# Decoder block on one NeuronCore: four buffers for the down product's integers, convolution sums split between POOL and DVE, the last tile turned on PE, and a new table of wanted times

## The chip, the core and the metric

The kernel runs on one core of a Trainium2 chip. Its engines work side by side, each through its own queue of instructions in a fixed order: PE (matrix products and transposes, results to PSUM), DVE and POOL (elementwise work), ACT (activations, copies, scaling) and SP, which here issues every DMA. POOL works on SBUF alone; DVE and ACT read PSUM too. An instruction starts when it is at the head of its queue and the semaphores it waits for have been raised.

The metric is the device time of one execution in microseconds (us), the median over runs.

## The reference

One decoder block on x of shape (16, 256, 512), in float32. Cut to what matters:

```python
x = x + attn(layernorm(x))            # 16 heads of 32, causal, q/k/v/o projections with bias
x = x + long_conv(ctx, ctx, layernorm(x))   # pairs of ctx rows convolved with a kernel of 512 taps
x = x + ffn(layernorm(x))             # 512 -> 2 x 1408 -> 512, quantized

def quant_dequant(v):                 # per row, for x, h and both weights
    scale = max(max|v| / 127, 1e-8)
    return clip(round(v / scale), -127, 127) * scale
# ffn: gate, up = split(xq @ w1q.T); h = silu(gate) * up; out = quant_dequant(h) @ w2q.T
```

The convolution treats the 16 batches as the long axis and the layer works on 32 groups of 8 channels ("heads" hh, two in each tile). In the quantized part the values that go into the products are small integers, held exactly in bfloat16; "integers" in what follows means these.

## The kernel before

**Order.** Nothing is scheduled by the compiler. Each step of the work (a function with a handful of instructions on one engine) is handed to a planner, class `Plan`, by `pl.add(key, engine, when, took, fn, ...)`: its engine, the time at which it is wanted, a cost, the steps that it comes after (`after`, data; `then`, order only), and the buffers that it takes (`new`) and uses (`use`). `order()` walks through time: whenever an engine is free it starts, of the steps that are ready and whose buffers have room, the one wanted earliest. The list that comes out is the program, and so the order of every engine's queue. The number of buffers of each kind stands in `Plan(...)`; `hq=2` is the ring of the down product's integers. The wanted times are simple formulas, to which the table `shift` adds a correction by kind of step and by stretch of the plan; the stretches are divided at 60, 330, 570, 680 and 1010.

**Attention.** 64 units (16 batches, 4 groups of heads). For each batch the layernorm is split into two half-precision parts, `xh` and `xl` (POOL), which SP turns by DMA transposes (`turn_out`). For each unit PE makes the q and k projections in three products (L617 to L619); ACT and DVE split them again (L725, L730); SP stores them and loads the stacked heads; PE makes the scores (L759), DVE the row extremes (L768), ACT the exponentials (L775), PE transposes (L800) and weighs. Beside this, POOL, ACT and SP prepare the pair products of the convolution (L905, L918, L923) and the integer weights of the quantized part.

**Convolution and quantized part.** 32 tiles of 128 rows, i = 0 to 31 (`NT` is 32). For each half-tile h of a tile, `conv_mm` multiplies on PE (L321 to L323), `conv_mul` multiplies on DVE into one of three buffers `u` (L335, L338, L341), and `conv_sum` adds up in three steps: n = 0, three adds inside `u` (L350, L352, L353); n = 1, three adds into the single buffer `vsum` (L355 to L357); n = 2, one add into `oT` (L361). Steps n = 0 and 1 run on POOL, step 2 on DVE for h = 0 and for the first three tiles, else on POOL. `conv_back` transposes `oT` (PE, L367), `conv_out` adds it to the residual `x2` (DVE, L373). Then comes a norm over ACT, DVE and POOL (L261, L265, L269, L277, L282), the row maximum (DVE, L379 to L381), rounding and casting (ACT, L386, L388) to `xb`, and `ffn_flip`: one DMA transpose from SP to `xq` (L393).

The quantized part of a tile goes through four blocks of columns (384, 384, 384, 256): gate product (PE, L407), scaling (DVE, L414), silu (ACT, L418), times the up scales (L425, on POOL in two halves, for the last two tiles on DVE), up product (PE, L407), times the gate (DVE, L432), row maximum (DVE, L436), its inverse (`up_inv`, four small DVE instructions, L444 to L447), rounding (`up_round`, ACT, L451), casting to `hb` (`up_cast`, ACT, L457), turning by DMA transpose to `hq` (`up_flip`, SP, L463), the down product (PE, L469), its scale and the residual (L478, L487 on DVE; for tiles 28 to 30, `LATE`, L476 on ACT and L483, L484 on POOL), and the store (L491). The last tile (31, `e` in the code) does silu, maximum, rounding, casting and turning block by block, with four DMA transposes; the other tiles do each in one piece.

## Time and profile before

| | us |
|---|---|
| median of three runs | 1176.3 |
| lowest and highest run | 1174.56, 1177.24 |
| the profiled execution, its own time | 1177.95 |
| its span, first to last instruction | 1176.1 |
| POOL add n = 0 (L350, L352, L353), mean of each | 1.278, 0.737, 0.730 |
| POOL add n = 1 (L355, L356, L357), mean of each | 0.937, 0.931, 0.390 |
| the add of n = 2 on POOL (L361), mean | 0.726 |
| the same add on DVE, least, median, most | 0.406, 0.426, 1.477 |
| DMA transpose to landing, xq and hq, median | 2.4, 4.1 |

The profiled execution is a single one, and every duration below is from it; its mean granted TensorE clock is 0.986. Busy shares are averages over stages that differ: attention up to about 631 us (the last transposes at L800 start at 630.9), the convolution and the quantized part after it. A matmul's row carries the length of one instruction; they are pipelined, so 12 gate products of 384 columns take 1.95 us and 11 down products 2.37 us.

### The profile page before, as it was taken

How to read it: one execution, taken by the hardware profiler on the slowest of the kernel's cores; microseconds unless marked ns; L12 is line 12 of the kernel's file. 1: busy time of each engine (PE TensorE's matmuls, PEld its weight loads, DVE VectorE, ACT ScalarE, POOL GpSimd, SP SyncE). 2: the span in 40 equal slices, each digit the busy share in tenths (PEclk: the TensorE clock that was granted, in tenths of full speed). 3: DMA queues.
4: the chain of work that ended last, by engine and by line, in shares of the span. 5: the costliest groups of instructions: out<-in, count | busy, mean ns of one | idle time of the engine just before them, and what ended most of it. 6: DMA issues, size and time to landing. Idle time of an engine off the chain costs nothing.

```text
span 1176.1 us, 25549 instructions
## 1 busy us (share of the span) xinstructions
PE 1083.6 (92%) x8488; PEld 767.0 (65%) x8488; DVE 989.7 (84%) x3165; ACT 839.8 (71%) x2001; POOL 957.2 (81%) x939
## 2 busy tenths in 40 slices
PE   4889989999999999998999999999999999999975
PEld 3666757767667666676666766676776777676632
DVE  5998778888788787886777879999999999999975
ACT  5878878888998888898875455556656665655454
POOL 2585988989899979879513889999999999999971
PEclk9999989999999999999999999999999999999988
DMA  6687787889888779887638855656776667766323
GB/s 223 165 203 230 222 220 231 252 233 242 222 260 230 243 209 260 237 234 213 169 117 291 292 156 156 189 155 186 182 182 165 176 167 171 170 184 177 77 60 69
DMA packets 271106, 229.97 MB, mean 196 GB/s; under 512 B 127257, under 2 KB 225599, under 8 KB 270847
## 3 DMA queue, kind: packets, MB, share of 16 engines
q1 hardware_dynamic: 270975, 228.35, 69.8%
q8 instruction: 67, 1.10, 0.4%
q14 instruction: 64, 0.52, 0.1%
HBM read 124.10 MB, written 75.74 MB: 170 GB/s over the span
## 4 chain that ended last, share of the span: by engine, by line
PE 50%; DVE 20%; ACT 11%; DMA 10%; POOL 4%; issue 3%; SPq 1%; POOLq 0%; ACTq 0%; DVEq 0%
PE g L407 8%; PE c L321 5%; PE c L323 5%; PE c L322 5%; PE d L469 4%; ACT p L775 4%; PE pj_qk L618 3%; PE pj_qk L617 3%; PE pj_qk L619 3%; DMA xlT<-xl 3%; DVE p L768 2%; DVE u L335 2%; DVE s L436 2%; PE pt L800 2%; PE s L759 2%
## 5 line engine op out<-in xcount | busy, mean ns | idle before, releaser
L775 ACT ACTIVATE p<-p,nmax 128x256 f32<-128x256 f32 (+1 forms) x512 | 229.9, 455 | 6.2 <-DVE nmax L768 6.1
L768 DVE CUSTOM_DVE_ANT_0 p<-s,mask,esc 128x128 f32<-128x128 f32 (+1 forms) x512 | 188.1, 410 | 11.8 <-PE s L759 11.4
L321 PE MATMUL c<-bkv,T 128*128 128x288 f16 x640 | 183.9, 287 | 9.4 <-DVE u L341 5.8
L323 PE MATMUL c<-bkv,T 128*128 128x288 f16 x640 | 183.8, 287 | 0.0
L322 PE MATMUL c<-bkv,T 128*128 128x288 f16 x640 | 183.8, 287 | 0.0
L407 PE MATMUL g<-w,xq 128*128 128x384 bf16 (+1 forms) x1024 | 171.5, 313 | 6.4 <-DVE hp L432 3.0
L923 POOL TENSOR_TENSOR kv<-p,kv 128x1152 f16<-128x1152 f32 x64 | 152.0, 2382 | 13.3 <-ACT kv L918 13.1
L905 POOL TENSOR_TENSOR p<-kT 128x1024 f32<-128x1024 f32 x64 | 143.8, 2248 | 2.6
L407 PEld LDWEIGHTS <-xq 128*128 128x128 bf16 x1024 | 99.8, 98 | 58.9 <-issue 7.2
L425 POOL TENSOR_TENSOR g<-g,sw 128x704 f32<-128x704 f32 x60 | 100.6, 1698 | 8.2 <-ACT g L418 8.2
L775 ACT ACTIVATION_READ_ACCUMULATOR p<-p,nmax 128x1 f32 x512 | 101.0, 197 | 0.0
L759 PE MATMUL s<-st 96*128 96x128 f16 (+1 forms) x512 | 85.1, 247 | 13.9 <-DVE nmax L768 10.1
L335 DVE TENSOR_TENSOR u<-c,qT 128x512 f32<-128x512 f32 x128 | 87.4, 682 | 11.3 <-PE c L323 9.0
L730 DVE SCALAR_TENSOR_TENSOR qkhl<-pj_qk,bias,qkhl 128x256 f16<-128x256 f32 x128 | 59.7, 478 | 40.2 <-ACT qkhl L725 30.8
L725 ACT ACTIVATE qkhl<-pj_qk,bias 128x256 f16<-128x256 f32 x128 | 60.1, 470 | 45.9 <-PE pj_qk L619 38.0
L469 PE MATMUL d<-w,hq 128*128 128x512 bf16 x352 | 85.8, 393 | 7.7 <-DVE s L445 4.3
L451 ACT ACTIVATE hp<-hp,s 128x1408 f32<-128x1408 f32 (+2 forms) x35 | 47.7, 1369 | 54.2 <-DVE s L447 54.1
L350 POOL TENSOR_TENSOR u<-u 128x512 f32<-128x512 f32 x64 | 81.8, 1278 | 5.4 <-DVE u L335 5.4
L321 PEld LDWEIGHTS <-T 128*128 128x128 f16 x640 | 62.8, 98 | 29.1 <-DVE u L341 7.7
L800 PE MATMUL pt<-idf,p 128*128 128x128 f32 x520 | 79.7, 277 | 2.3 <-ACT t L808 1.3
L918 ACT CAST kv<-p 128x1152 f16<-128x1152 f32 x64 | 73.5, 1149 | 11.0 <-POOL p L909 5.9
L786 POOL TENSOR_SCALAR lb<-lsum 128x256 f32<-128x256 f32 x64 | 26.0, 406 | 64.1 <-DVE lsum L782 40.0
(220 smaller groups left out, 3323.9 us busy)
## 6 DMA issues: line engine op xcount, KB each, us to landing
kv_d<-kv SPq DMA_DIRECT2D x64, 576.0 KB, 4.1
bkv<-kv_d SPq DMA_DIRECT2D x64, 576.0 KB, 4.1
qk_d<-qkhl SPq DMA_DIRECT2D x64, 256.0 KB, 3.3
st<-qk_d SPq DMA_DIRECT2D x256, 64.0 KB, 2.5
T<-pad_d SPq DMA_DIRECT2D x64, 256.0 KB, 5.0
x_d<-xt SPq DMA_DIRECT2D x32, 256.5 KB, 3.6
bx<-x_d SPq DMA_DIRECT2D x32, 256.5 KB, 3.9
xt<-in_x_dram SPq DMA_DIRECT2D x16, 512.0 KB, 4.0
```

The lines of the kernel that those rows point to most:

```text
L321: nc.tensor.matmul(reg, T[:, 0, d:d + P], kv[:, mi, 0, :], start=mi == 0, stop=False)
L322: nc.tensor.matmul(reg, T[:, 0, d:d + P], kv[:, mi, 1, :], start=False, stop=False)
L323: nc.tensor.matmul(reg, T[:, 1, d:d + P], kv[:, mi, 0, :], start=False, stop=mi == li)
L335: nc.vector.tensor_tensor(ap(u, uo, [[UW, 2], [64, 4], [1, 64]]), ap(pc, 0, [[512, 2], [64, 4], [1, 64]]), ap(qT, qo, [[96, 2], [8, 4], [1 ...
L407: nc.tensor.matmul(pg[:, :c.stop - c.start].rearrange("p (r o) -> p r o", o=P), t["xq"][:, kc, :], w1[:, (o + c.start) // P:(o + c.stop) / ...
L469: nc.tensor.matmul(pd.rearrange("p (r o) -> p r o", o=P), t["hq"][:, ic, :], w2[:, :, ic, :], start=ic == 0, stop=ic == IC - 1)
L759: nc.tensor.matmul(ps[:, hh, :nk], stk[:, 0, 2 * h2 + hh, qc * P:(qc + 1) * P], stk[:, 1, 2 * h2 + hh, :nk], start=True, stop=True)
L768: nc.vector.tensor_tensor_reduce(out=prs[b, g][qc][:, h, :], in0=ps[:, hh, :nk], in1=mask2[:, P - qc * P:2 * P], op0=ALU.add, op1=ALU.min, ...
L775: nc.scalar.activation(pr[:, h, :], pr[:, h, :], AF.Exp, scale=-1.0, bias=nmax[:, qc, h:h + 1], accum_out=lsum[:, qc, h:h + 1])
L800: nc.tensor.transpose(pt[:, j, :], src, idf)
L905: nc.gpsimd.tensor_tensor(ap(p, 0, [[NKV, 4], [64, 4], [1, 64]]), ap(kT, o, [[96, 4], [0, 4], [1, 64]]), ap(kT, o, [[96, 4], [8, 4], [1, 6 ...
L923: nc.gpsimd.tensor_tensor(kv[:, :, 1, :], p, kv[:, :, 0, :], ALU.subtract)
```

## The change

Four things. The ring of `hq` has four buffers instead of two. `conv_sum` asks a function `sum_on` for its engine: step n = 0 of the second half-tile of tiles 0 to 3 goes from POOL to DVE, and step n = 1 of the last half-tile too; when n = 0 and n = 1 are on different engines, n = 1 no longer waits for n = 0. In the last tile, the input's integers and the down product's are turned by transposes on PE into PSUM and copied to SBUF, instead of by DMA; of the four column blocks the odd ones are rounded, cast and copied on DVE, the even ones on ACT. The table of wanted times is replaced as a whole (the boundaries stay), and the bias maximum at the start is wanted later. A bfloat16 identity is made at the start.

```diff
@@ -147,6 +147,8 @@
 
     idf = cst.tile([P, P], F32, name="idf")
     make_identity(nc, idf)
+    idb = cst.tile([P, P], BF16, name="idb")
+    nc.vector.tensor_copy(idb, idf)
 
     mask2 = cst.tile([P, 2 * P], F32, name="mask2")
     nc.gpsimd.memset(mask2, 0.0)
@@ -195,6 +197,7 @@
     NT = len(tiles)
     UB = 3
     LATE = range(NT - 4, NT - 1)
+    EARLY = 4
 
     ts = [dict() for _ in tiles]
 
@@ -342,9 +345,13 @@
             ap(u, uo + 256, [[UW, 2], [32, 2], [1, 32]]), ap(pc, 256, [[512, 2], [0, 2], [1, 32]]),
             ap(qT, qo + 32, [[96, 2], [32, 2], [1, 32]]), ALU.mult)
 
+    def sum_on(i, h, n):
+        dve = (n == 2 and (h == 0 or i < 3)) or (n == 0 and h and i < EARLY) or (n == 1 and h and i == NT - 1)
+        return "DVE" if dve else "POOL"
+
     def conv_sum(i, h, n):
         u = ts[i]["u", h]
-        g = nc.gpsimd
+        g = nc.gpsimd if sum_on(i, h, n) == "POOL" else nc.vector
         if n == 0:
             a = ap(u, 0, [[UW, 4], [1, 128]])
             g.tensor_tensor(a, a, ap(u, 128, [[UW, 4], [1, 128]]), ALU.add)
@@ -358,7 +365,7 @@
         else:
             if h == 0:
                 ts[i]["oT"] = cv.tile([P, 4, P], F32, tag="oT", bufs=3, name=f"oT{i}")
-            (g if h and i > 2 else nc.vector).tensor_tensor(ts[i]["oT"][:, :, 64 * h:64 * h + 64], ap(u, 0, [[UW, 4], [1, 64]]), vs[:, :, 0:64], ALU.add)
+            g.tensor_tensor(ts[i]["oT"][:, :, 64 * h:64 * h + 64], ap(u, 0, [[UW, 4], [1, 64]]), vs[:, :, 0:64], ALU.add)
 
     def conv_back(i):
         t = ts[i]
@@ -386,6 +393,17 @@
         nc.scalar.activation(xn, xn, AF.Copy, bias=RND, scale=t["s"][:, 1:2])
         t["xb"] = ff.tile([P, D], BF16, tag="xb", bufs=2, name=f"xb{i}")
         nc.scalar.activation(t["xb"], xn, AF.Copy, bias=-RND)
+
+    def ffn_turn(i):
+        t = ts[i]
+        t["pt"] = ps_sd.tile([P, 512], BF16, tag="sd", name=f"sd_x{i}")
+        for kc in range(KC):
+            nc.tensor.transpose(t["pt"][:, kc * P:(kc + 1) * P], t["xb"][:, kc * P:(kc + 1) * P], idb)
+
+    def ffn_keep(i):
+        t = ts[i]
+        t["xq"] = ff.tile([P, KC, P], BF16, tag="xq", bufs=5, name=f"xq{i}")
+        nc.vector.tensor_copy(t["xq"].rearrange("p k s -> p (k s)"), t["pt"])
 
     def ffn_flip(i):
         t = ts[i]
@@ -448,18 +466,41 @@
 
     def up_round(i, n):
         t, c = ts[i], parts(i)[n]
-        nc.scalar.activation(t["hp"][:, c], t["hp"][:, c], AF.Copy, bias=RND, scale=t["s"][:, 3:4])
+        if n % 2:
+            nc.vector.tensor_scalar(t["hp"][:, c], t["hp"][:, c], t["s"][:, 3:4], RND, ALU.mult, ALU.add)
+        else:
+            nc.scalar.activation(t["hp"][:, c], t["hp"][:, c], AF.Copy, bias=RND, scale=t["s"][:, 3:4])
 
     def up_cast(i, n):
         t, c = ts[i], parts(i)[n]
         if n == 0:
             t["hb"] = ff.tile([P, I], BF16, tag="hb", bufs=2, name=f"hb{i}")
-        nc.scalar.activation(t["hb"][:, c], t["hp"][:, c], AF.Copy, bias=-RND)
+        if n % 2:
+            nc.vector.tensor_scalar(t["hb"][:, c], t["hp"][:, c], -RND, None, ALU.add)
+        else:
+            nc.scalar.activation(t["hb"][:, c], t["hp"][:, c], AF.Copy, bias=-RND)
+
+    def up_turn(i, n):
+        t, c = ts[i], parts(i)[n]
+        if n == 0:
+            t["pt"] = ps_c.tile([P, 2048], BF16, tag="c", name=f"c_h{i}")
+        for j in range(c.start, c.stop, P):
+            nc.tensor.transpose(t["pt"][:, j:j + P], t["hb"][:, j:j + P], idb)
+
+    def up_keep(i, n):
+        t, c = ts[i], parts(i)[n]
+        if n == 0:
+            t["hq"] = ff.tile([P, IC, P], BF16, tag="hq", bufs=4, name=f"hq{i}")
+        dst = t["hq"].rearrange("p r s -> p (r s)")[:, c]
+        if n % 2:
+            nc.vector.tensor_copy(dst, t["pt"][:, c])
+        else:
+            nc.scalar.copy(dst, t["pt"][:, c])
 
     def up_flip(i, n):
         t, c = ts[i], parts(i)[n]
         if n == 0:
-            t["hq"] = ff.tile([P, IC, P], BF16, tag="hq", bufs=2, name=f"hq{i}")
+            t["hq"] = ff.tile([P, IC, P], BF16, tag="hq", bufs=4, name=f"hq{i}")
         nc.sync.dma_start_transpose(t["hq"][:, c.start // P:c.stop // P, :], t["hb"][:, c])
 
     def down_mm(i):
@@ -1032,11 +1073,11 @@
         T = 8.8
         pl = Plan(xt=XB, xn=1, xh=2, xl=2, xhT=2, xlT=2, v=2, pj=2, qk=3, st=STB, s=2, pr=2, lb=2, pt=3, tt=2, av=1,
                   lt=2, ah=2, ct=1, cr=2, kT=2, p=2, kv=2, qw=3, qb=2, qt=2, x1=5, q=2, qT=4, sd=1, kv2=3, c=2, u=UB, oT=3, x2=8, xn2=2, xb=2, xq=5, ac=3,
-                  g1=3, hp=2, hb=2, hq=2, o1=2)
+                  g1=3, hp=2, hb=2, hq=4, o1=2)
 
         pl.add("bi", "SP", -100, 1.1, bias_in, late=2.0, dma=0.3)
         pl.add("bm", "PE", -99, 0.1, bias_turn, late=0.2, after=["bi"], new=[("pt", "b")])
-        pl.add("bx", "DVE", -98, 0.7, bias_max, late=0.1, after=["bm"], use=[("pt", "b")])
+        pl.add("bx", "DVE", -66, 0.75, bias_max, late=0.1, after=["bm"], use=[("pt", "b")])
         for n, nm in enumerate(names):
             j = n // 2
             pl.add(("pi", nm), "SP", -80 + 10 * n, 0.55, proj_in, nm, late=1.5, dma=3.3)
@@ -1260,8 +1301,9 @@
                            after=[("cm", hh, l2), ("bk", i, 1), ("cz", hh % UB)], then=[("cu", hh, 0) if l2 else ("cu", hh - 1, 1)],
                            new=[u] * (1 - l2), use=[c, u, qT])
                 for n in range(3):
-                    pl.add(("cs", hh, n), "DVE" if n == 2 and (h == 0 or i < 3) else "POOL", w + 6 + 2.5 * n, (2.85, 2.37, 0.69 if h else 0.45)[n], conv_sum, i, h, n, late=0.08,
-                           after=[("cu", hh, 1)] if n == 0 else [("cs", hh, n - 1)], then=[("cs", hh - 1, 2)],
+                    on = sum_on(i, h, n)
+                    pl.add(("cs", hh, n), on, w + 6 + 2.5 * n, ((2.85, 2.37, 0.69) if on == "POOL" else (2.3, 2.0, 0.45))[n], conv_sum, i, h, n, late=0.08,
+                           after=[("cu", hh, 1)] + [("cs", hh, m) for m in range(n) if n == 2 or sum_on(i, h, m) == on], then=[("cs", hh - 1, 2)],
                            new=[oT] * (n == 2 and h == 0), use=[u] + [oT] * (n == 2))
             pl.add(("co", i), "PE", t + 22, 0.44, conv_back, i, late=0.2, after=[("cs", 2 * i + 1, 2)], new=[("sd", ("o", i))], use=[oT])
             pl.add(("cx", i), "DVE", t + 23, 0.67, conv_out, i, late=0.1, after=[("co", i), "ff"], new=[x2], use=[("sd", ("o", i)), x1])
@@ -1269,7 +1311,11 @@
             root(i, "f", t + 24, [("cx", i)], xn, 0.1)
             pl.add(("fm", i), "DVE", t + 27, 0.98, ffn_top, i, late=0.1, after=[("fq", i)], use=[xn, x2])
             pl.add(("fo", i), "ACT", t + 28, 1.29, ffn_round, i, late=0.1, after=[("fm", i)], new=[("xb", i)], use=[xn])
-            pl.add(("ft", i), "SP", t + 30, 1.23, ffn_flip, i, late=1.2, dma=0.8, after=[("fo", i)], new=[("xq", i)], use=[("xb", i)])
+            if e:
+                pl.add(("fd", i), "PE", t + 30, 0.35, ffn_turn, i, late=0.2, after=[("fo", i)], new=[("sd", ("x", i))], use=[("xb", i)])
+                pl.add(("ft", i), "DVE", t + 30.5, 0.45, ffn_keep, i, late=0.1, after=[("fd", i)], new=[("xq", i)], use=[("sd", ("x", i))])
+            else:
+                pl.add(("ft", i), "SP", t + 30, 1.23, ffn_flip, i, late=1.2, dma=0.8, after=[("fo", i)], new=[("xq", i)], use=[("xb", i)])
             xq, g1, hp, hb, hq, o1 = ("xq", i), ("g1", i), ("hp", i), ("hb", i), ("hq", i), ("o1", i)
             g = t + (34 if e else 38)
             np = NC if e else 1
@@ -1286,12 +1332,18 @@
                        after=[("gm", i, 1, n), ("gu", i, n if e else 0)], then=[("um", i, 0)] * (n > 0), new=[hp] * (n == 0), use=[("ac", (i, 1, n)), g1, hp])
             for n in range(np):
                 pl.add(("gl", i, n), "ACT", g + 7 + n, 1.37 * k + 0.16 * e, gate_silu, i, n, late=0.1, after=[("gs", i, n if e else NC - 1)], use=[g1])
-                pl.add(("gu", i, n), "POOL" if i < NT - 2 else "DVE", g + 8 + n, (3.4 if i < NT - 2 else 1.5 + 0.3 * e) * k, gate_ups, i, n, late=0.05,
+                pl.add(("gu", i, n), "POOL" if i < NT - 2 else "DVE", g + 8 + n, (3.3 if i < NT - 2 else 1.5 + 0.3 * e) * k, gate_ups, i, n, late=0.05,
                        after=[("gl", i, n), ("fv", 1)], use=[g1])
                 pl.add(("ut", i, n), "DVE", g + 15 + n, 1.54 * k + 0.08 * e, up_top, i, n, late=0.1, after=[("um", i, n if e else NC - 1)], use=[hp])
-                pl.add(("uq", i, n), "ACT", g + 18 + n, 1.37 * k + 0.15 * e, up_round, i, n, late=0.1, after=[("ui", i)], use=[hp])
-                pl.add(("ub", i, n), "ACT", g + 19 + n, 1.28 * k + 0.1 * e, up_cast, i, n, late=0.1, after=[("uq", i, n)], new=[hb] * (n == 0), use=[hp, hb])
-                pl.add(("uf", i, n), "SP", g + 20 + n, 1.2 if e else 1.45, up_flip, i, n, late=1.2, dma=2.1 * k, after=[("ub", i, n)], new=[hq] * (n == 0), use=[hb, hq])
+                q = "DVE" if n % 2 else "ACT"
+                pl.add(("uq", i, n), q, g + 18 + n, 0.35 if n % 2 else 1.37 * k + 0.15 * e, up_round, i, n, late=0.1, after=[("ui", i)], use=[hp])
+                pl.add(("ub", i, n), q, g + 19 + n, 0.35 if n % 2 else 1.28 * k + 0.1 * e, up_cast, i, n, late=0.1, after=[("uq", i, n)], then=[("ub", i, 0)] * (n > 0), new=[hb] * (n == 0), use=[hp, hb])
+                if e:
+                    c = ("c", ("h", i))
+                    pl.add(("ud", i, n), "PE", g + 20 + n, 0.28, up_turn, i, n, late=0.2, after=[("ub", i, n)], then=[("ud", i, n - 1)], new=[c] * (n == 0), use=[hb, c])
+                    pl.add(("uf", i, n), q, g + 20.5 + n, 0.4, up_keep, i, n, late=0.1, after=[("ud", i, n)], then=[("uf", i, 0)] * (n > 0), new=[hq] * (n == 0), use=[c, hq])
+                else:
+                    pl.add(("uf", i, n), "SP", g + 20 + n, 1.45, up_flip, i, n, late=1.2, dma=2.1, after=[("ub", i, n)], new=[hq] * (n == 0), use=[hb, hq])
             pl.add(("ui", i), "DVE", g + 17, 0.76 + 0.2 * e, up_inv, i, late=0.1, after=[("ut", i, n) for n in range(np)], use=[x2])
             pl.add(("dm", i), "PE", g + 25, 2.38, down_mm, i, late=0.2, after=[("uf", i, n) for n in range(np)] + [("fw", 4)],
                    new=[("ac", (i, 2))], use=[hq])
@@ -1305,102 +1357,104 @@
 
         bounds = (60,330,570,680,1010)
         shift = {-            ("bi", 2): (-7.9, -13.9, -6, -15.4, -13.3, -3.2),
-            ("bk", 3): (4.3, -0.6, -0.5, -0.8, -0.8, 0.9),
...
+            ("bi", 2): (0.8, 5.7, 3, 5.9, 1.9, 8.6),
+            ("bk", 3): (14.4, 12.2, -4.6, 11.1, 15.6, 13.5),
...
```

## The prediction

> **What bounds the kernel now.** I read the busy shares first, then the busy time by stage, then the tail engine by engine in order of time, then the waits of PE. Busy shares over the whole span:
>
> ```profile
> PE 1083.6 (92%) x8488; PEld 767.0 (65%) x8488; DVE 989.7 (84%) x3165; ACT 839.8 (71%) x2001; POOL 957.2 (81%) x939
> ```
>
> PE is idle for 1176.1 - 1083.6 = 92.5 us. The stages (columns: stretch, length, then busy time and instructions of PE, PEld, DVE, ACT, POOL, granted clock, DMA share, GB/s) say where:
>
> ```profile
> 0.00:60.00 60.00, 39.22 (x294) 31.27 (x295) 43.30 (x148) 42.32 (x85) 24.53 (x29) 1.00 0.67 194
> 60.00:200.00 140.00, 127.67 (x1103) 91.43 (x1102) 117.11 (x446) 116.72 (x354) 114.51 (x93) 0.98 0.77 221
> 200.00:330.00 130.00, 124.23 (x1084) 89.86 (x1083) 108.14 (x424) 117.67 (x359) 119.30 (x95) 1.00 0.86 239
> 330.00:450.00 120.00, 111.26 (x964) 80.55 (x963) 97.34 (x381) 106.23 (x312) 108.96 (x89) 1.00 0.83 235
> 450.00:570.00 120.00, 110.76 (x960) 79.00 (x959) 92.09 (x352) 101.03 (x294) 101.38 (x79) 0.99 0.78 224
> 840.00:920.00 80.00, 79.65 (x573) 56.47 (x572) 75.13 (x195) 48.81 (x68) 76.47 (x88) 1.00 0.67 172
> 1100.00:1140.00 40.00, 33.34 (x199) 19.89 (x198) 32.69 (x80) 22.09 (x26) 33.46 (x38) 0.91 0.26 51
> 1140.00:1176.00 36.00, 21.86 (x108) 10.08 (x106) 21.28 (x49) 15.26 (x22) 9.81 (x8) 0.89 0.29 64
> ```
>
> Between 840 and 920 PE is busy 99.6%: there nothing that leaves PE's work as it is can help. The idle time sits in the start (20.8 us), in attention (60 to 570: 510 - 473.9 = 36.1 us), in 620 to 760 (10.5 us: 140 less 129.5), and in the tail, 1100 to 1176 (20.8 us). The tail in order of time (start, length, what; in brackets the idle time before and its cause):
>
> ```profile
> 1135.79 0.74 DVE L373 SCALAR_TENSOR_TENSOR x<-sd_o,rsall,bx 128x512 f32<-128x512 f32 x1
> ...
> 1160.36 0.21 DVE L447 TENSOR_SCALAR s<-s 128x1 f32<-128x1 f32 x1
> 1170.33 0.76 DVE L478 SCALAR_TENSOR_TENSOR d<-d,s,sw 128x512 f32<-128x512 f32 x1 [9.76 <-PE d L469]
> 1171.60 0.69 DVE L487 TENSOR_TENSOR o<-d,x 128x512 f32<-128x512 f32 x1 [0.51 <-DMA out_dram<-o]
> ```
>
> From the last tile's residual (1136.45) to its inverse maximum (1160.57) DVE idles 2 us of 24.1: DVE bounds this piece. From 1160.57 to 1170.33 everything waits on one chain. ACT and PE show it:
>
> ```profile
> 1161.89 1.11 ACT L451 ACTIVATE hp<-hp,s 128x384 f32<-128x384 f32 x2
> 1162.90 0.93 ACT L457 ACTIVATE hb<-hp 128x384 bf16<-128x384 f32 x2
> 1163.72 1.01 ACT L451 ACTIVATE hp<-hp,s 128x384 f32<-128x384 f32 x2
> 1164.63 0.82 ACT L457 ACTIVATE hb<-hp 128x384 bf16<-128x384 f32 x2
> ```
> ```profile
> 1169.69 0.60 PE L469 MATMUL d<-w,hq 128*128 128x512 bf16 x2 [0.51 <-DMA hq<-hb]
> ```
>
> ACT ends casting at 1165.45, but PE ends at 1170.29: 4.8 us are DMA transposes landing one behind the other.
>
> **Part 1, the last turn (tail after 1160.57).** Before: 1176.1 - 1160.57 = 15.5 us. Now, from the inverse on: two roundings and two casts on ACT, 1.11 + 0.93 = 2.0, while DVE does the other four (its nearest row is L414, 128x384 in 0.55, so at most 2.2). Then ACT has tile 30's o1 scale (0.67) in front of its copies; the 11 transposes (four of L367 take 0.60 to 0.66, so about 1.7) run meanwhile, behind the down products of tiles 29 and 30. Two copies on ACT: between 0.37 (128x256, L841) and 0.57 (128x512, L808), say 0.47 each, 0.95. Hops between engines, four at about 0.1: 0.4. Last three down products 0.82. Sum 4.9, then the same end as before: 0.76 + 0.69, and 3.8 from 1172.29 to the end of the span. That gives 10.2; I take 11.0, since tile 29's scale stood before the roundings for 1.3 us and may again. Gain 4.5; bounds: 2.0 (that wait stays, and all 11 products wait for the last copy, 1.6 more) and 5.3. The stores of tiles 29 and 30 leave SP earlier than before, as six DMA transposes are gone from its queue; the ring of two o1 buffers held the last add 0.5 us before and can again. The input's turn (one DMA transpose, median 2.4 to landing, against 0.66 + 0.69 for transposes and copy, L810) I cost at nothing: DVE has over 10 us of queue before that copy. Without this cover it gains 1.0.
>
> **Part 2, the tail before 1160.57.** The new order of the queues puts more of tiles 28 to 30 ahead of the last tile. Counting DVE's queue between x2 of tile 31 and its inverse, at this trace's durations (four scalings 1.8, four products with the gate 1.75, the up scales 1.65 or 1.75, a row maximum 1.53, an inverse 0.76, norm maximum 1.0): before 22.1 us, after 19.4 with the new copy of 0.6, since tile 29's and 30's scalings and a quarter of tile 29's products have moved ahead of x2. Idle was 2.0; I allow 2.5, as the last tile now runs more alone. That is 24.1 to 21.9, a gain of 2.2. Ahead of it POOL, from the last add of n = 2 on DVE (1109.77 before) to the end of oT31 (1134.53), has 24.8 us before and, counted from its new queue, 22.3 (one step n = 1 less; 11 us of up scales stay). DVE has about 24 in the same stretch, so only 0.8 of it counts. Gain 3.0; bounds -1 (DVE's two extra SBUF adds each held, below) and 6 (POOL's and DVE's savings in full, no new idle time).
>
> **Part 3, tiles 0 to 3.** Four steps n = 0 leave POOL: 4 x (1.28 + 0.74 + 0.73) = 11.0 us. On DVE the three adds take at least 0.68 + 0.41 + 0.41 = 1.5 (L335 for 512 elements, L361 for 256), so 6 us. But the same add on DVE takes two lengths:
>
> ```profile
> 652.23 1.39 DVE L361 TENSOR_TENSOR oT<-u,vsum 128x256 f32<-128x256 f32 x1
> 664.26 0.43 DVE L361 TENSOR_TENSOR oT<-u,vsum 128x256 f32<-128x256 f32 x1
> ```
> ```profile
> 652.08 1.26 POOL L350 TENSOR_TENSOR u<-u 128x512 f32<-128x512 f32 x1
> 663.13 1.27 POOL L350 TENSOR_TENSOR u<-u 128x512 f32<-128x512 f32 x1
> ```
>
> The long one started just behind a POOL add and ended with it; the short one started as another POOL add was ending (664.40). So each of the 12 moved adds can be held by up to 1.0 us: DVE pays 6 to 18 us, and between 640 and 720, where these tiles run, it has 14.9 us idle (POOL 10, PE 6.6). PE's own waits for `u` are 4.3 us here. I take a gain of 1.0; bounds -4 (18 less 14.9, and conv_mul, which PE waits for, queued behind the held adds) and 4 (those 4.3 us).
>
> The Trainium skill's page "SBUF — State Buffer", section "Who interferes with whom", says more than these rows: a DVE instruction with two SBUF inputs and a POOL instruction that reads SBUF exclude each other for a whole instruction. Then POOL too stands still during the moved adds and wins only half of what it hands over; by that rule this part would be worth nothing, and the total one microsecond less.
>
> **Part 4, four hq buffers.** Nothing. No row of SP's waits names the down product as what held a transpose; PE's 3.4 us of waiting for hq are all in the last tile. Bounds 0 and 1.
>
> **Part 5, the new order elsewhere.** Attention has the same instructions. On PE's queue I counted, at the trace's pitches, the work between a unit's last projection and its first score: median 17.6 us before, 17.0 after, least 9.7 and 8.9; between last score and first transpose 6.0 and 6.6. Nothing separates the two orders. At the start the second batch's input is loaded and split earlier, but k's norm comes behind one more cast (1.0): I allow a gain of 1. For the rest the four stretches between 60 and 570 show how far one order varies: PE idles 8.8, 4.4, 7.3 and 7.7%, a scatter of 1.9%, which is 2.4 us in a stretch and 4.8 over four independent ones. Value 1.0, bounds -9 and 11 (two scatters each way).
>
> **Sum.** 4.5 + 3.0 + 1.0 + 0 + 1.0 = 9.5. The profiled execution took 1177.95 (span 1176.1, 1.85 around it), so 1168.5 for it; it stands 1.65 above the median, so 1167 for a median.
>
> **The rivals.**
> - *Slower: the new order starves the projections.* In attention the longest kind of DMA wait is this:
>
> ```profile
> PE pj_qk L618 <- DMA xlT<-xl: 6.4, 7, 2.3
> ```
>
> 6.4 us in 7 waits, the longest 2.3. If the 15 batches after the first all wait the longest, that is 34.5, 28 more. It decides from (9.5 + 2.4 + 6.4) / 15 = 1.2 us in each batch; half way between that point and the worst the time would be 1167 + 20 = 1187. For it: SP's queue is one, and every store moved ahead of the xl transpose delays PE. Against it: the number of units still to be stored behind that transpose averages 0.7 before and 1.0 after, no worse. Chance 0.20.
> - *No change: the tail keeps its length.* DVE stays the bound, its held adds and the longer idle time of a lone last tile eat part 2, part 1 gives its 2.0 and the rest cancels: 1176.3 - 2.0 = 1174 to 1176. For it: DVE is already at 88% from 1135 to 1161. Against it: the DMA landings do go. Chance 0.10, half of it within 0.2%.
> - *Faster still: the order also fills attention.* If all of 60 to 570 idled as the best stretch does (4.4%), 36.1 would become 22.7, and 1167 - 13.4 = 1153. For it: one stretch does it with POOL and ACT over 90% busy. Against it: the counts above. Chance 0.20.
>
> **How the numbers follow.** Forecast 1167 with 0.50. Its own range: half bounds of 1.7, 3.5, 4 and 7 (0.8 of part 5's) add in squares to 9, so 1158 to 1176. The full range takes in the faster rival and about a third of the slower: 1153 to 1182. A measurement here can tell about 0.2%, 2.4 us. Faster: 0.50 less 0.02, 0.20, and 0.05 of the middle rival, 0.73; within 0.2%: 0.02 and 0.05, 0.07; slower 0.20.
>
> **What would show it.** From the last tile's inverse to the end of the span 10 to 12 us instead of 15.5 (part 1; wrong if over 13.5), from its x2 to the inverse 20 to 23 instead of 24.1 (part 2), the moved adds on DVE with lengths spread from 0.4 to 1.5 (part 3), no wait gone at SP (part 4), PE's busy time between 60 and 570 within 5 us of 473.9 (part 5). The prediction is wrong if PE's idle time in attention moves by more than 12 us, or if DVE from 640 to 720 has no idle time left and PE's waits for `u` grow.

## The result and the profile after

The changed kernel takes 1159.65 us (median of four runs, 1158.62 to 1164.23), the kernel before 1176.49 in the same session: a ratio of 0.9867 with a 95% interval of [0.9837, 0.9896], some 16 us. The profiled execution of after took 1164.23, the longest of its four; its span is 1162.4 us against 1176.1, and the mean granted clock 0.993 against 0.986. The busy shares over the span, then the same stages as before (columns as in the prediction):

```profile
PE 1076.4 (93%) x8503; PEld 766.8 (66%) x8503; DVE 1015.8 (87%) x3188; ACT 838.0 (72%) x1999; POOL 947.5 (82%) x924
```
```profile
0.00:60.00 60.00, 42.30 (x316) 33.97 (x317) 43.92 (x160) 45.33 (x92) 27.03 (x30) 1.00 0.69 203
60.00:200.00 140.00, 128.36 (x1106) 91.72 (x1104) 118.31 (x446) 119.55 (x362) 117.83 (x95) 0.99 0.83 225
200.00:330.00 130.00, 125.35 (x1104) 91.86 (x1102) 109.30 (x426) 117.38 (x355) 118.87 (x96) 1.00 0.82 236
330.00:450.00 120.00, 109.99 (x959) 79.32 (x958) 98.25 (x388) 102.49 (x305) 101.30 (x83) 0.99 0.85 237
450.00:570.00 120.00, 114.84 (x997) 82.38 (x995) 95.23 (x365) 107.92 (x320) 108.79 (x85) 1.00 0.82 234
840.00:920.00 80.00, 79.30 (x565) 55.54 (x563) 75.93 (x193) 46.34 (x63) 75.25 (x87) 1.00 0.64 173
1100.00:1140.00 40.00, 27.49 (x159) 15.80 (x156) 37.43 (x81) 20.32 (x23) 22.75 (x24) 0.91 0.20 41
1140.00:1162.00 22.00, 13.57 (x76) 6.72 (x76) 14.83 (x31) 9.16 (x15) 7.69 (x6) 0.94 0.36 80
```

PE does 3.1 us more in the first 60 us and 4.6 more between 60 and 570 (478.5 against 473.9). From 840 to 920 it stays busy 99.1%, against 99.6. In the tail DVE is now the full engine: 37.4 of 40 us, where it had 32.7. PE's 27.5 against 33.3 is no loss of work: the span is 13.7 us shorter, so this window lies nearer to its end; in the 40 us that end 36 us before the end of each span PE is busy 32.3 and was 33.3, and DVE 37.8 and was 32.7.

Landmarks tell better than shares where the 13.7 us between the spans come from. Each is the start of a named instruction, in us:

| | before | after | gain |
|---|---|---|---|
| first unit weighed (first DVE write of `al`; L853, now L894) | 63.5 | 60.4 | 3.1 |
| last unit weighed | 636.3 | 624.2 | 12.1 |
| first conv matmul (L321, now L324) | 633.7 | 621.6 | 12.1 |
| last conv matmul, counted from the first | 482.2 | 481.5 | 0.7 |
| last inverse (first instruction), counted from the last conv matmul | 43.6 | 45.9 | -2.3 |
| end, counted from that inverse | 16.6 | 13.4 | 3.2 |

So nearly all of it is won before the convolution starts, the long middle is as it was, and the tail gives back in front of the inverse most of what it wins behind it. The tail on DVE, in order of time (start, length, what): the last residual, the end of the last inverse, the last down product's scale and residual.

```profile
1128.81 0.74 DVE L380 SCALAR_TENSOR_TENSOR x<-sd_o,rsall,bx 128x512 f32<-128x512 f32 x1
...
1149.85 0.21 DVE L465 TENSOR_SCALAR s<-s 128x1 f32<-128x1 f32 x1
...
1156.99 0.76 DVE L519 SCALAR_TENSOR_TENSOR d<-d,s,sw 128x512 f32<-128x512 f32 x1 [1.16 <-PE d L510]
1157.84 0.69 DVE L528 TENSOR_TENSOR o<-d,x 128x512 f32<-128x512 f32 x1
```

From the inverse's end (1150.06) to the span's end are 12.3 us, where there were 15.5. From the residual (ends 1129.48) to the inverse's end are 20.6, where there were 24.1. The residual itself, however, ends 26.4 us after the start of the last conv matmul, where it ended after 20.5.

PE's waits between 60 and 560 us (us in total, times, longest) do not get shorter everywhere:

```profile
PE pj_qk L659 <- DMA xlT<-xl: 10.7, 6, 3.7
PE pj_qk L658 <- ACT qkhl L766: 6.9, 9, 1.1
PE s L800 <- DVE nmax L809: 6.6, 14, 1.7
```

The wait for the transposed `xl` rose from 6.4 to 10.7 us, the one for ACT's `qkhl` from 4.8 to 6.9, and the one for `nmax` fell from 8.4 to 6.6; the rows that went are many small ones (the wait for the stacked heads `st` was 2.0, for DVE's `t` 2.0 and 1.1, for `qkhl` on DVE 2.3, now 1.0).

### The profile page after: what moved, and what is told of

It is laid out like the page before. It is cut to its first block, busy times and chain, and to the rows that moved or that the text cites. A ratio compares the mean times of both kernels' runs of the same rounds, so it can differ in the third digit from the quotient of the medians.

```text
span 1162.4 us, 25593 instructions
## 1 busy us (share of the span) xinstructions
PE 1076.4 (93%) x8503; PEld 766.8 (66%) x8503; DVE 1015.8 (87%) x3188; ACT 838.0 (72%) x1999; POOL 947.5 (82%) x924
## 4 chain that ended last, share of the span: by engine, by line
DVE 32%; PE 31%; POOL 13%; ACT 9%; DMA 8%; issue 5%; SPq 2%; DVEq 0%; POOLq 0%; ACTq 0%
DVE hp L450 4%; PE g L425 4%; ACT p L816 3%; DVE s L454 3%; DVE u L338 3%; DVE p L809 3%; PE pj_qk L659 3%; PE pj_qk L658 3%; PE pj_qk L660 3%; DMA xlT<-xl 2%; DVE u L341 2%; PE c L324 2%; PE c L326 2%; PE c L325 2%; POOL g L443 2%
## 5 line engine op out<-in xcount | busy, mean ns | idle before, releaser
L816 ACT ACTIVATE p<-p,nmax 128x256 f32<-128x256 f32 (+1 forms) x512 | 230.0, 454 | 11.3 <-DVE nmax L809 10.7
L324 PE MATMUL c<-bkv,T 128*128 128x288 f16 x640 | 183.2, 286 | 9.4 <-issue 3.2
L425 PE MATMUL g<-w,xq 128*128 128x384 bf16 (+1 forms) x1024 | 169.1, 315 | 13.1 <-DVE o L528 6.3
L771 DVE SCALAR_TENSOR_TENSOR qkhl<-pj_qk,bias,qkhl 128x256 f16<-128x256 f32 x128 | 59.9, 478 | 33.5 <-ACT qkhl L766 21.0
L357 POOL TENSOR_TENSOR u<-u 128x512 f32<-128x512 f32 x60 | 76.9, 1282 | 9.6 <-DVE u L338 9.6
L510 PE MATMUL d<-w,hq 128*128 128x512 bf16 x352 | 80.9, 379 | 3.8 <-DVE hp L450 3.0
L324 PEld LDWEIGHTS <-T 128*128 128x128 f16 x640 | 62.6, 98 | 29.1 <-DVE u L344 5.9
L659 PE MATMUL pj_qk<-xlT,wq_hi 128*128 128x256 f16 x256 | 70.5, 275 | 10.7 <-DMA xlT<-xl 10.7
L658 PE MATMUL pj_qk<-xhT,wk_hi 128*128 128x256 f16 x256 | 70.0, 273 | 7.3 <-ACT qkhl L766 6.9
```

The source lines that it names most:

```text
L324: nc.tensor.matmul(reg, T[:, 0, d:d + P], kv[:, mi, 0, :], start=mi == 0, stop=False)
L425: nc.tensor.matmul(pg[:, :c.stop - c.start].rearrange("p (r o) -> p r o", o=P), t["xq"][:, kc, :], w1[:, (o + c.start) // P:(o + c.stop) / ...
L658: nc.tensor.matmul(ps, lh, rh, start=first, stop=False)
L659: nc.tensor.matmul(ps, lh, rl, start=False, stop=False)
L816: nc.scalar.activation(pr[:, h, :], pr[:, h, :], AF.Exp, scale=-1.0, bias=nmax[:, qc, h:h + 1], accum_out=lsum[:, qc, h:h + 1])
```

## The experiments

Each run stands beside runs of the kernel before on the same chip. The table has the ratio to that kernel, and from the profiled execution the start of the first conv matmul, the length of the conv stretch (first to last conv matmul), the way from the last conv matmul to the first instruction of the last inverse, and from there to the end.

| run | ratio and 95% interval | first conv | conv stretch | to inverse | to end |
|---|---|---|---|---|---|
| before | 1 | 633.7 | 482.2 | 43.6 | 16.6 |
| after | 0.9867 [0.9837, 0.9896] | 621.6 | 481.5 | 45.9 | 13.4 |
| e1_old_table | 1.0204 [1.0175, 1.0233] | 631.5 | 499.0 | 52.3 | 14.7 |
| e2_table_only | 1.0056 [1.0034, 1.0079] | 614.5 | 504.9 | 45.0 | 15.9 |
| e3_sum_pool | 0.9871 [0.9849, 0.9894] | 619.0 | 481.4 | 46.0 | 13.4 |
| e4_dma_last | 0.9892 [0.9873, 0.9911] | 614.2 | 481.9 | 45.9 | 16.6 |
| e5_attn_table | 1.0072 [1.0049, 1.0096] | 615.2 | 500.9 | 48.3 | 15.9 |
| e6_new_conv | 1.0166 [1.0149, 1.0183] | 633.5 | 497.7 | 49.2 | 14.4 |
| e7_early_on_pool | 0.9860 [0.9838, 0.9882] | 615.2 | 481.7 | 46.7 | 13.3 |
| e8_ring_two | 0.9876 [0.9827, 0.9926] | 619.9 | 479.8 | 46.7 | 13.3 |
| e9_order_only | 0.9901 [0.9869, 0.9934] | 616.1 | 481.6 | 46.3 | 16.6 |
| e10_tail_new | 0.9849 [0.9825, 0.9873] | 617.7 | 479.6 | 42.8 | 14.2 |
| e11_tail_two | 0.9800 [0.9777, 0.9822] | 615.2 | 479.4 | 40.8 | 12.4 |
| e12_start_only | 0.9962 [0.9939, 0.9985] | 627.6 | 482.0 | 43.3 | 16.6 |

### The table of wanted times, whole and in parts

e1 gives the changed kernel the old table:

```diff
-            ("bi", 2): (0.8, 5.7, 3, 5.9, 1.9, 8.6),
+            ("bi", 2): (-7.9, -13.9, -6, -15.4, -13.3, -3.2),
...
```

> The changed kernel with the wanted times of the kernel before (its shift table; steps new in the change get no shift); all else as changed. Theory (the new order of start and attention brings some 12 us of the 13.7 between the profiled spans): 1170 to 1177 us, and the first conv matmul starts within 4 us of the 633.7 of before, against 621.6 after. Rival (the early sums on DVE, the ring of four or the turn on PE bring the gain): 1158 to 1163, with the first conv matmul near 622. The old table was made for other steps, so a time above 1180 speaks against neither.

Measured: 1198.6 us. The first conv matmul is at 631.5, as the theory said; but the conv stretch grew by 17 us, which neither theory had (a time above 1180 had been allowed for, as speaking against neither). e2 is the other half, the kernel before with the new table (the same lines the other way round):

> The kernel before with the new wanted times alone: no sum moved, two buffers for the down product's integers, the last tile turned by DMA. Theory (the table's first stretches bring some 12 us): 1162 to 1167 us, first conv matmul between 619 and 625. Rival (the table needs the other parts with it): 1172 to 1180, first conv matmul above 629.

Measured: 1181.15 us. Attention gains even more than in the changed kernel, 614.5 against 633.7 before, and the conv stretch loses 22.7 us. So in both, attention's length follows the table, and the total does not: the theory's total was wrong by 14 us or more. e5 and e6 divide the table by its columns, that is by stretches of the plan.

```diff
# e5, in the kernel before: three new columns, three old ones
-            ("bi", 2): (-7.9, -13.9, -6, -15.4, -13.3, -3.2),
+            ("bi", 2): (0.8, 5.7, 3, -15.4, -13.3, -3.2),
...
# e6, in the changed kernel: three old columns, three new ones
-            ("bi", 2): (0.8, 5.7, 3, 5.9, 1.9, 8.6),
+            ("bi", 2): (-7.9, -13.9, -6, 5.9, 1.9, 8.6),
...
```

> The kernel before with the new wanted times in the table's first three columns alone (planned times below 570); the three later columns, the sums, the ring and the last tile's transfers as before. Theory (the new order of start and attention is worth 12 to 19 us by itself, and the later columns fit only the code that they were made for): first conv matmul between 613 and 622 against 633.7, conv stretch 480 to 484 us as before, so 1156 to 1165 us. Rival (attention's gain needs the later columns too, or is given back in the conv stretch as in the run with the whole table): first conv matmul above 628, or a conv stretch above 490, and 1172 to 1185 us.

> The changed kernel with the first three columns of the old table and the last three of the new one. Theory (the early columns are the gain, the later ones fit the moved sums): first conv matmul 629 to 634, conv stretch 480 to 485 us, end 58 to 60 us after the last conv matmul, so 1168 to 1176 us. Rival (the conv stretch's order was fitted to the new order of attention, too): a conv stretch above 488 us, and 1177 to 1195.

Measured: 1186.41 and 1196.95 us. Attention is at 615.2 with the new early columns and at 633.5 with the old ones, in whichever code. The conv stretch is long again in both, 500.9 and 497.7: here the rivals were right, though both times came out just above their ranges. Where the conv stretch loses, PE waits longer for DVE's products into `u`, which read the conv product's PSUM buffer and so free it. Two views: the conv matmuls of e5 with their first and last start, and PE's waits over e5's conv stretch.

```profile
L321 PE MATMUL c<-bkv,T x640: 282/286/448, 615.2 to 1116.1; 128*128 128x288 f16 x160
```
```profile
PE c L321 <- DVE u L341: 10.9, 8, 3.8
PE c L321 <- DVE rn_f L265: 5.0, 3, 2.5
```

The same wait in the kernel before, on which e5 is built, and in the changed kernel, each over its own conv stretch:

```profile
PE c L321 <- DVE u L341: 5.8, 8, 1.4
```
```profile
PE c L324 <- DVE u L344: 3.2, 4, 1.8
```

10.9 us against 5.8 and 3.2, and 5.0 more that the profile puts down to an instruction of DVE's norm. In e1, e2 and e6 this wait is 9.8, 10.7 and 11.6 us. In e5 the two rows make up 10 of the 19 us; the rest is spread over smaller ones.

e12 changes the first column alone in the kernel before:

> The kernel before with the new wanted times in the table's first column alone (planned times below 60): the start's order, with the old columns behind it. Read by the first conv matmul, since a mixed table costs the conv stretch 15 to 23 us in every run so far. Theory (the start brings the 3 us by which the first unit is earlier, the columns of attention the rest): first conv matmul at 629 to 632 us against 633.7 before and 615 with three new columns. Rival (the start's order sets the rhythm of the units, and all of the gain comes from it): 613 to 622. The time: 1175 to 1200 either way.

Measured: 1170.68 us, first conv matmul at 627.6, 6.1 us earlier, between the two cases and nearer the theory; the first unit is weighed at 59.9 against 63.5, so 3.6 of the 6.1 are there by 60 us. The times agree: 0.9962 [0.9939, 0.9985] is 2 to 7 us, and not all of the gain. (e12 keeps the bias maximum where it was and has no second identity, so the start's gain is not theirs.) The assumption in the expectation, that a mixed table always costs the conv stretch, is wrong: 482.0. Counting in the programs fits this. Of DVE's 741 steps of the convolution and the quantized part, e12 has none in another order than the kernel before; e5 has 333 out of their old order, e2 420, and the changed kernel itself 380. All kernels in which this part has the complete order of before, or of after, have a conv stretch of 479 to 482 us; the four new mixtures have 498 to 505. Why these two orders are good and four others bad was not tried.

e9 keeps the changed kernel's order and undoes its other parts in their places:

```diff
# e9
-        g = nc.gpsimd if sum_on(i, h, n) == "POOL" else nc.vector
+        g = nc.gpsimd if sum_on(i, h, n) == "POOL" or n < 2 else nc.vector
...
-        if n % 2:
+        if False:
...
-            if e:
+            if False:
                 pl.add(("fd", i), "PE", ...)
...
-tag="hq", bufs=4
+tag="hq", bufs=2
```

> The changed kernel with all of its other parts undone in their places: the early sums and the last middle sum on POOL, two buffers for the integers, the last tile rounded on ACT and turned by DMA; the order of the work is the changed kernel's wherever the steps are the same. Theory (the whole gain is the order's, 12 us of it ahead of the first conv matmul, and the three other parts together bring at most 4 us): 1160 to 1166 us, first conv matmul 613 to 622, conv stretch 480 to 484 us. Rival (the parts each bring something that the others cover when one is undone alone): above 1168 us.

Measured: 1162.31 us, ratio 0.9901 [0.9869, 0.9934], first conv matmul 616.1, conv stretch 481.6, each as the theory said. 1.0% of the 1.33% (11.6 of some 16 us; by the interval 8 to 15) is the order's. This is the run that settles where the gain comes from; that it comes before the conv stretch is e1, e2, e5 and e6 together.

### The last tile's turn

e4 undoes the turn on PE, as in e9, and with it the split of the last tile's rounding and casting (all four blocks on ACT again); the sums and the ring stay as changed.

> The changed kernel with the last tile's integers of both products turned by DMA as before, all blocks rounded and cast on ACT, ring of four and all else kept. Theory (the turn on PE saves 3 us after the inverse and 3.5 before it): 5 to 7 us slower than the changed kernel, 1165 to 1167, with 15 to 16 us from the start of the last inverse to the end, against 12.3, and 23.5 to 24.5 from x2 to the inverse, against 20.6. Rival (the tail's order, not the transfer, sets these lengths): 0 to 2 us slower, the two lengths within 1 us of the changed kernel's.

Measured: 1161.49 us, 0.25% above the changed kernel, about 2.9 us, with intervals that overlap. The lengths show it clearly. (The expectation's 15 to 16 and 12.3 are counted from the inverse's end, not from its start.) From the inverse's end to the end of the span 15.5 us against 12.3; from the residual to the inverse's end 20.6 in both. The split brings none of it: the last cast ends 4.2 us behind the inverse in e4, with all blocks on ACT, and 4.1 in the changed kernel. So the turn of the down product's integers is worth 3.2 us, and the turn of the input nothing. PE at the end of e4, and at the end of after:

```profile
1146.99 0.82 PE L510 MATMUL d<-w,hq 128*128 128x512 bf16 x3 [2.54 <-DMA hq<-hb]
1149.31 2.74 PE L510 MATMUL d<-w,hq 128*128 128x512 bf16 x6 [1.49 <-DMA hq<-hb]
1152.53 0.60 PE L510 MATMUL d<-w,hq 128*128 128x512 bf16 x2 [0.49 <-DMA hq<-hb]
```
```profile
1151.69 0.34 PE L488 MATMUL c_h<-idb,hb 128*128 128x128 bf16 x3 [0.24 <-ACT hb L481]
1152.97 0.51 PE L488 MATMUL c_h<-idb,hb 128*128 128x128 bf16 x6 [0.94 <-DVE hb L479]
1154.24 0.29 PE L488 MATMUL c_h<-idb,hb 128*128 128x128 bf16 x2 [0.76 <-DVE hb L479]
1154.37 2.58 PE L510 MATMUL d<-w,hq 128*128 128x512 bf16 x11
```

In e4 the down products wait three times for a transfer (2.54, 1.49, 0.49). In after the turns wait for the casts on DVE (0.94, 0.76), which end late for a reason of their own: the rows of DVE and of POOL there.

```profile
1150.10 2.54 DVE L470 TENSOR_SCALAR hp<-hp,s 128x384 f32<-128x384 f32 x2
1152.57 1.62 DVE L479 TENSOR_SCALAR hb<-hp 128x384 bf16<-128x384 f32 x2
```
```profile
1149.88 1.27 POOL L524 TENSOR_TENSOR o<-o,sw 128x512 f32<-128x512 f32 x1 [6.83 <-ACT o L517]
1151.23 1.27 POOL L525 TENSOR_TENSOR o<-o,x 128x512 f32<-128x512 f32 x1
1152.70 1.34 POOL L524 TENSOR_TENSOR o<-o,sw 128x512 f32<-128x512 f32 x1 [0.20 <-ACT o L517]
```

Two roundings take 2.54 us and two casts 1.62; the first pair ends (1152.64) 0.14 us behind POOL's second add, the second pair (1154.19) 0.15 behind its third. One by one they take 1.27, 1.36, 0.35 and 1.35 us: three are long, and the first cast, which starts at 1152.57 in the gap between POOL's second and third add, is not. e10 below has no POOL add beside them and shows their own length.

### The sums

e3 puts the last n = 1 back on POOL, e7 the four early n = 0; e8 gives the ring two buffers.

```diff
# e3
-        g = nc.gpsimd if sum_on(i, h, n) == "POOL" else nc.vector
+        g = nc.gpsimd if sum_on(i, h, n) == "POOL" or n == 1 else nc.vector
# e7
+        g = nc.gpsimd if sum_on(i, h, n) == "POOL" or n == 0 else nc.vector
# e8
-tag="hq", bufs=4
+tag="hq", bufs=2
```

> The changed kernel with the middle sum (n = 1) of the last half tile issued on POOL instead of DVE, at the same place of the order. Theory (that sum and the o sum before it, held to 5.9 us together on DVE while POOL adds, cost the tail 2 to 5 us): 1155 to 1158 us, PE's wait of 6.0 us ahead of the gate product shrinks below 3.5 and the last x2 comes within 24.5 us of the end of the last conv product, against 26.1. Rival (POOL, which then does 2.3 us more ahead of the last n = 0 sums, is as late): within 1 us of the changed kernel, or slower.

Measured: 1158.02 us, ratio 0.9871, no difference from the changed kernel's 0.9867; the rival was right. What the theory saw is there. DVE, POOL and PE in the changed kernel (start, length, what):

```profile
1113.81 1.89 DVE L368 TENSOR_TENSOR oT<-u,vsum 128x256 f32<-128x256 f32 x1
1115.73 1.87 DVE L362 TENSOR_TENSOR vsum<-u 128x352 f32<-128x352 f32 x1
1117.64 1.47 DVE L363 TENSOR_TENSOR vsum<-vsum,u 128x352 f32<-128x352 f32 x1
1119.14 0.66 DVE L364 TENSOR_TENSOR vsum<-vsum 128x96 f32<-128x96 f32 x1
```
```profile
1113.73 3.49 POOL L443 TENSOR_TENSOR g<-g,sw 128x704 f32<-128x704 f32 x2
1117.18 1.54 POOL L357 TENSOR_TENSOR u<-u 128x512 f32<-128x512 f32 x1
1118.80 0.88 POOL L359 TENSOR_TENSOR u<-u 128x256 f32<-128x256 f32 x1
```
```profile
1121.25 5.61 PE L425 MATMUL g<-w,xq 128*128 128x384 bf16 x24 [6.02 <-DVE o L528]
```

Four DVE adds take 5.9 us beside POOL's, and PE stands still for 6.02 until DVE gets to tile 27's residual. In e3, PE:

```profile
1114.06 3.21 PE L425 MATMUL g<-w,xq 128*128 128x384 bf16 x20 [2.01 <-DVE o L528]
...
1123.34 1.12 PE L374 MATMUL sd_o<-idf,oT 128*128 128x128 f32 x4 [3.33 <-POOL oT L368]
```

That wait is 2.01, but 9 us later PE waits 3.33 for `oT` from POOL, which now does n = 1, and tile 29's up scales (3.3 us) before the last sum. The residual starts 24.1 us after the last conv matmul instead of 25.7, but to the inverse it is 46.0 against 45.9: one wait took the place of the other.

> The changed kernel with the first sums (n = 0) of the first four tiles' second halves issued on POOL again, everything else in the same order. Theory (those sums are 2.2 to 4.3 us each on DVE, held by POOL, but spare POOL 2.85 us each while the early tiles are behind on POOL; their effect on the end is small): within 2 us of the changed kernel, 1157 to 1163. Rival one (POOL was the bound there): 4 to 11 us slower, by up to 4 x 2.85. Rival two (the held sums on DVE stalled the conv products): 2 to 4 us faster, 1155 to 1158.

Measured: 1161.1 us, ratio 0.9860; no difference, as the theory said. The stretch from 640 to 720 (columns as above), first after, then e7:

```profile
640.00:720.00 80.00, 71.17 (x533) 52.23 (x531) 77.07 (x185) 41.23 (x62) 68.48 (x81) 1.00 0.71 205
```
```profile
640.00:720.00 80.00, 71.99 (x524) 52.18 (x522) 69.12 (x176) 42.13 (x62) 74.24 (x89) 0.98 0.65 187
```

On DVE the early sums cost 8 us there and spare POOL 5.8, and PE is as busy either way. (The windows hold nine of the twelve moved adds, and e7's convolution began 6.4 us earlier, so they show not quite the same work.)

> The changed kernel with two buffers for the down product's integers instead of four; the order of every engine stays the same. Theory (no transfer waited for a buffer): within 1.5 us of the changed kernel, 1157 to 1162, and the conv stretch between 480 and 484 us. Rival (the ring lets the transposing transfers run ahead, and so hides them): 3 us slower or more, 1163 or above, with a wait of SP for the down product.

Measured: 1162.05 us, ratio 0.9876; no difference that its interval of [0.9827, 0.9926] shows, conv stretch 479.8, and no wait of SP for the down product.

### A tail written out by hand

e10 keeps the changed kernel up to its last 120 steps, and gives these in a new order, with the last n = 1 and tile 30's up scales on POOL, tiles 29 and 30 finished on DVE, and two buffers for `hq` again:

```diff
-            for s in pl.order():
+            seq = pl.order()
+            tail = [('cs', 63, 2), ('gu', 29, 0), ('gm', 30, 0, 1), ('ut', 28, 0), ...]
+            for s in seq[:-len(tail)] + [pl.by[k] for k in tail]:
...
-        m = c.start + (c.stop - c.start) // (2 if i < NT - 2 else 1)
+        m = c.start + (c.stop - c.start) // (2 if i < NT - 1 else 1)
...
-        if i in LATE:
+        if i == NT - 4:
...
-tag="hq", bufs=4
+tag="hq", bufs=2
...
-tag="o1", bufs=2
+tag="o1", bufs=4
```

> The changed kernel with its last 120 steps in an order written out by hand: the last middle sum on POOL, the last o sum ahead of tile 29's product on POOL, tile 30's product on POOL in two halves, the last tile's root and turn ahead of the down products, the two last down products scaled and added on DVE after the last roundings; ring of two for the integers, four output tiles. Theory (the 46 us from the last conv product to the last inverse hold some 5 us that DVE spends held by POOL or waiting behind POOL and PE's order, and the roundings after it another 2): 39 to 42 us from conv to inverse, 11 to 12 after it, so 4 to 8 us faster than the changed kernel, 1152 to 1156. Rival (DVE is full there whatever the order): 45 to 46 us from conv to inverse and within 2 us of the changed kernel's time.

Measured: 1156.27 us, ratio 0.9849, at the upper edge of what was expected: 42.8 us to the inverse, just outside the 39 to 42, and 14.2 after it, not 11 to 12. (The interval overlaps the changed kernel's.) DVE and PE of e10, the rows that matter:

```profile
1135.13 0.56 DVE L450 TENSOR_TENSOR hp<-g,g 128x384 f32<-128x384 f32 x1 [2.58 <-ACT hb L481]
...
1141.18 0.68 DVE L470 TENSOR_SCALAR hp<-hp,s 128x384 f32<-128x384 f32 x2
1141.78 0.55 DVE L479 TENSOR_SCALAR hb<-hp 128x384 bf16<-128x384 f32 x2
```
```profile
1138.73 6.47 PE L510 MATMUL d<-w,hq 128*128 128x512 bf16 x22 [1.76 <-DMA hq<-hb]
```

Without a POOL add beside them the two roundings take 0.68 and the two casts 0.55, 1.2 us for what took 4.2. But DVE idles 2.58 us before the last tile's up product, whose buffer `hp` waits for tile 29's rounding and cast on ACT, and the down products of tiles 29 and 30 wait 1.76 for a transfer and hold the turns behind them. e11 moves that rounding up:

```diff
# e11, against e10
-('ui', 29), ('gm', 31, 0, 1), ... ('gm', 31, 1, 1), ('uq', 29, 0), ('ub', 29, 0), ('uf', 29, 0), ...
+('ui', 29), ('uq', 29, 0), ('ub', 29, 0), ('uf', 29, 0), ('gm', 31, 0, 1), ... ('gm', 31, 1, 1), ('uq', 30, 0), ...
```

> The kernel of the hand-written tail with one thing moved: the roundings of tiles 29 and 30 on ACT come as soon as their scales are there, ahead of the last tile's silu blocks and of tile 28's scaling. Theory (DVE's one long wait of that tail, 2.58 us ahead of the last tile's up product, is for the buffer that tile 29's rounding frees, and the last down products wait 1.76 us for a transfer that starts with the same roundings): conv to inverse 39 to 41 us against 42.8, inverse to end 12 to 13.5 against 14.2, so 2 to 4 us faster, 1152 to 1154 us. Rival (the silu blocks of the last tile, now up to 2.9 us later on ACT, hold DVE as long): within 1 us of the run before, or slower.

Measured: 1149.71 us (median of five), ratio 0.9800 [0.9777, 0.9822], all below the changed kernel's interval: 40.8 us to the inverse, 12.4 after it. DVE's wait at that place:

```profile
1130.82 0.56 DVE L450 TENSOR_TENSOR hp<-g,g 128x384 f32<-128x384 f32 x1 [0.91 <-PE g L425]
```

0.91 instead of 2.58, now for PE. This is the fastest version; it beats the kernel before by 2.0% and the changed kernel by some 8 to 10 us. The lengths of the tail explain 6.1 us of that (53.2 against 59.3 from the last conv matmul to the end), and 3.8 of the 6.6 by which its median lies below e10's, which is more than was expected; in its profiled execution attention, in the same order, was 2.5 us shorter too.

## Why the prediction came out as it did

The forecast, faster with 1167 us, was right in sign, and 1159.65 lies in the range; it is 7 us below the forecast, because two terms of the sum were far off, in opposite directions. That the number came so near is in part luck: the tail was to bring 7.5 of the 9.5 us and brought 0.9, and the term put at 1.0 brought 12.1.

**Part 5, the new order elsewhere (1.0 predicted): the term that was mis-sized.** Between the profiled executions it is 12.1 us, and e9 has 11.6 for the order alone, its 2.7 us longer way to the inverse included. The step that failed is "Nothing separates the two orders". It compared the median work on PE's queue between a unit's last projection and its first score (17.6 and 17.0 us), and a median does not show what PE loses in single places. Up to the first conv matmul PE has the same 4917 instructions in both kernels and is idle 60.8 us before and 51.6 after, so 9.2 of the 12.1 are idle time that went:

```profile
0.00:633.70 633.70, 572.89 (x4917) 413.77 (x4918) 508.13 (x1944) 535.00 (x1579) 480.96 (x398) 0.99 0.78 222
```
```profile
0.00:621.60 621.60, 570.03 (x4917) 413.61 (x4918) 508.25 (x1945) 535.02 (x1579) 480.80 (x398) 0.99 0.80 226
```

They are spread over many rows: the wait for DVE's `qkhl` fell from 4.5 to 1.0, that for `nmax` from 10.1 to 8.4, while that for `xlT` rose from 6.6 to 10.7. Which of the table's entries do it was not tried one by one. The gain grows over the whole of attention: unit 24 is weighed 5.5 us earlier, unit 48 8.2, the last 12.1. The start was allowed 1 and gives 3.1 by the first unit and, in e12, 6.1 by the first conv matmul. The bound of 11, from the scatter of the four stretches, was the better guide than the count, but it was too low: in the eight profiled executions with this order the convolution begins 12.1 to 19.5 us earlier than in the one of the kernel before, and the 12.1 is the least of them.

**Part 2, ahead of the residual (gain 0.8 predicted): wrong in sign.** It is a loss of 5.9 us. The count of POOL's and DVE's queues (22.3 and 24 us) was taken at unheld lengths, and the held adds were named only as a bound of -1. The four DVE adds took 5.9 us there, and PE waited 6.02. But the held adds were not the main cause. In e9 and e3, where POOL does that sum, the residual still starts 24.1 us after the last conv matmul, against 25.7 in the changed kernel and 19.9 before: 4.2 us come with the order alone, 1.6 with the adds on DVE, and at the inverse these 1.6 are gone (46.3 and 46.0 us, against 45.9). The length is set by DVE, POOL and PE's order together, and e10 and e11 get it down by moving all three.

**Part 2, from the residual to the inverse (24.1 to 21.9 predicted): right,** 20.6. But the two pieces share DVE's queue: where the residual comes 1.6 us earlier, this piece is 22.6 (e9) and 22.3 (e3). Only their sum can be judged, and it was forecast as a gain of 3.0 and is a loss of 2.3. That the input's turn is worth nothing behind DVE's queue was right too: 20.6 with the DMA transpose (e4), 20.6 without.

**Part 1, the last turn (4.5 predicted): right in kind, mis-sized.** 3.2, the rest is 12.3 instead of 11.0. The step was DVE's "at most 2.2" for two roundings and two casts, which took 4.2; with no POOL add beside them they take 1.2 (e10). The rule that bears on it is in the Trainium skill, page "SBUF — State Buffer", section "Who interferes with whom": it counts tensor_scalar among the DVE operations that can, when their operands meet its conditions, take the port pair shared with POOL, and says that whichever of the two was issued first then keeps it for the whole instruction and the other stands still. The rows agree: three of the four took 1.27, 1.36 and 1.35 us beside POOL's adds, against 0.42, 0.35 and 0.28 in e10, and the cast that started ahead of POOL's third add took its free 0.35. The prediction had weighed that section for adds with two SBUF inputs only.

**Part 3, the early sums (1.0 predicted): no effect that can be measured.** e7 without them is at 0.9860, against 0.9867. The moved adds' lengths (ns, least, median, most; first and last start), one row for each of the three adds:

```profile
L357 DVE TENSOR_TENSOR u<-u x4: 684/684/2156, 633.8 to 670.7; 128x512 f32<-128x512 f32 x4
```
```profile
L359 DVE TENSOR_TENSOR u<-u x4: 1035/1039/1045, 634.5 to 672.9; 128x256 f32<-128x256 f32 x4
```
```profile
L360 DVE TENSOR_TENSOR u<-u x4: 1032/1034/1037, 635.6 to 674.0; 128x256 f32<-128x256 f32 x4
```

The twelve take 12.5 us, inside the predicted 6 to 18, with lengths from 0.68 to 2.16 where 0.4 to 1.5 was named; the eight smaller ones are all held, to 1.03 or 1.04 us, where the same size takes 0.41 free. POOL is held as well: one of its n = 1 adds beside them took 1.31 us, where that add mostly takes 0.93.

```profile
634.49 1.04 DVE L359 TENSOR_TENSOR u<-u 128x256 f32<-128x256 f32 x1
```
```profile
633.94 1.31 POOL L362 TENSOR_TENSOR vsum<-u 128x352 f32<-128x352 f32 x1 [1.93 <-DVE oT L368]
```

This is what the skill's rule said of this part, worth 0 instead of 1.0; the runs can't tell these two apart.

**Part 4, four buffers (0 predicted): right,** e8. Two readings behind it were not quite right. SP's waits of the kernel before do name the down product, once:

```profile
SPq L463 <- PE d L469: 0.8, 1, 0.8
```

And of PE's 3.4 us for `hq` 1.25 belong to tile 30. Neither changes the value: with the last tile turned by DMA, two buffers (e9, where SP has one such row of 3.9 us) and four (e4, where it has none) take the same 16.6 us from the inverse on.

**The rivals.** Starving the projections moved the way it was feared, 6.4 to 10.7 us of waiting for `xlT`, but in 6 waits, 0.7 us for each of 15 batches, under the 1.2 from which it was to decide. The rival of a filled attention was nearer than its chance of 0.20 suggests: it had PE idle 22.7 us between 60 and 570; it was 31.5 in the profiled execution and 26.9 to 31.3 in the seven others where attention has the same order, against 36.1 before. The rival of an unchanged tail was right about the tail (43.6 + 16.6 = 60.2 us before, 59.3 after) and wrong in the end, since the gain came from elsewhere.

**The tests named.** PE's busy time between 60 and 570 stayed within 5 us of 473.9 (478.5), as it was to do if part 5 was right, and part 5 was wrong. That it stayed was chance: of the seven other executions with this order, six lie 6.7 to 9.2 us above 473.9, and one (e8) 4.8. A window that one order fills so differently can't decide. From the inverse to the end it took 12.3 us, above the 10 to 12 named and below the 13.5 from which part 1 was to be wrong.
